# Evidence and experts in two lines each, the router's parts added by a product, and a new plan table in a transformer block

## The chip, the cores and the metric

The kernel runs on one core of a Trainium2 chip. Five engines work side by side: TensorE (PE) multiplies matrices and writes its results to eight PSUM banks; VectorE (DVE) and ScalarE (ACT) work on tiles element by element and read PSUM; GpSimd (POOL) does the same on SBUF alone; SyncE (SP) issues the DMAs. The metric is the time of one execution in microseconds of device time. The kernel before takes 1758.62 us, the median of 3 runs (1758.21 to 1759.53).

## The reference, cut to what matters

Sixteen sequences of 256 tokens with 256 channels go through two layers. All is float32.

```python
# first layer: retrieval from the context, then three experts
nx = layer_norm(x) * gamma + beta
weights = softmax((nx @ Wq) @ (ctx @ Wk).T * 256 ** -0.5)
evidence = weights @ (ctx @ Wv)
combined = concat([nx, evidence, anchor])          # anchor: one vector per sequence
router_probs = softmax(combined @ router_W + router_b)          # 3 experts
h = silu(combined @ e_w1[e] + e_b1[e]);  expert_out[e] = h @ e_w2[e] + e_b2[e]
routed = sum over e of expert_out[e] * router_probs[e]
g = sigmoid(silu(combined @ gate_w1 + gate_b1) @ gate_w2 + gate_b2)
x = x + g * (routed @ out_w + out_b)

# second layer: each part on a normalised x, scaled and shifted by cond, its output gated
x = x + g_msa * self_attention(h)      # 16 heads of 16, windows of 128 rolled by 64
x = x + g_mca * top16_cross_attention(h, ctx)     # the 16 greatest of 256 scores, 16 heads
x = x + g_mlp * ((silu(h @ w_m1[:, :1024]) * (h @ w_m1[:, 1024:])) @ w_m2)
```

## The kernel before, in words

Weights lie in SBUF for the whole run; some are folded into one another first (`folds`, for instance the key weights into the query weights, and the value weights into the router's and the experts' first layers). Activations move through a ring of work buffers (`units`, 128x512 floats each: 26 at first, 76 once the setup's memory is given back by `settled`), a ring of small tiles (`smalls`) and the ring of the eight PSUM banks (`banks`).

The work of a sequence is written as eleven generators, the stages: `evidence` (norm, scores against the context, weights, the gathered evidence, and the router with its probabilities), `experts`, `self_keys`, `self`, `self_out`, `queries`, `keys`, `cross`, `cross_out`, `inputs` and `mlp`. Each yields operations (`Op`): an engine, a duration that the plan reckons with, the tiles that it reads, writes, takes and frees, and a function that issues its instructions. A stage has one line of work, in which it takes sequence 0, 1, 2 and so on (`line`, L1647); `mlp` has two lines, one for the even and one for the odd sequences (`every`, L1671). `after` in the table `STAGES` (L1625) says how far each stage may run ahead of others: `("experts", 2)` lets `evidence` of sequence b begin once `experts` of b - 2 is done. The other numbers of a row are a rank, the work buffers and banks that must stay free beside what a new operation takes, and a window: how many operations the line may have posted at once.

The order of the instructions on every engine is laid down at build time by a planner (`Flow.run`, L235). It keeps a clock for each engine and at each step takes, of all posted operations whose inputs are planned, the one that could begin first; between equals the one with the least time of readiness plus rank:

```python
if op.engine == PE:
    if self.tiled is None:
        rank += op.hold
    elif op.tiled:
        rank -= self.STAY
key = (begin + late, at + rank + late)
```

`tiled` marks the operations that use the array in quarters: the attention scores (`"rows"`, L1382 and L1516: four products of 32 rows at once), the weighted sums and the router's product (`"columns"`, L1337, L1482 and L1107: four products of 32 columns at once). Everything else uses the whole array: products (L565, L576, L1092) and transposes (L493, L1322, L1465, L1117). The planner adds `TURN` to an operation that changes between quarters and whole. While the array is quartered, `STAY` favours quartered operations; while it is whole, `HOLD` puts off the weighted sums. `ASIDE` is what an operation must gain to be moved to its second engine (a PSUM copy from ACT to DVE), `SWITCH` puts off work that needs another table of ACT.

The router's logits are made in parts. Its product (L1103) leaves four partial sums, one for each block of 128 input channels, on four groups of 32 partitions: partition 32k + e holds block k's part for expert e. ACT copies the result to SBUF (L1111), TensorE turns it in two transposes (L1117), VectorE adds the four parts straight from PSUM (`tensor_reduce`, L1133) and adds the router's bias (L1134); then the greatest logit, the shift, the exponential and the division follow (L1137 to L1150).

Sequences 0, 1 and 2 are loaded by the list of `fetches` between the weights; a later one is loaded by its `evidence` when it begins (L1053).

Of the kernel before, what the change touches and what calls it, by code (L numbers as in the profile page):

```python
# [11 lines left out]
ALU = mybir.AluOpType  # L12
AX = mybir.AxisListType
PSUM = bass.MemoryType.PSUM

P = 128
# [31 lines left out]
def t_tr(n):  # L48
    return n * 0.109
# [46 lines left out]
class Op:  # L96
# [5 lines left out]

    def __init__(
        self, engine, us, trace, r=(), w=(), new=(), free=(), table=None, size=0, tiled=None,
        other=(), grain=0.0, hold=0.0,
    ):
        self.hold = hold
# [19 lines left out]
class Flow:  # L127
# [4 lines left out]
    ASIDE = 1.0  # L132
    TURN = 0.093
    SWITCH = 3.0
    STAY = 8.0
    HOLD = 1.0
# [98 lines left out]
    def run(self):  # L235
        while self.works:
# [35 lines left out]
            if op.engine == PE:  # L272
                if (op.tiled is None) != (self.tiled is None):
                    us += self.TURN
                self.tiled = op.tiled
# [23 lines left out]
def pixart_kernel(  # L299
# [29 lines left out]
    for a in range(2):  # L329
        nc.vector.tensor_reduce(mask[:, a : a + 1], iv[:, :, a * D : (a + 1) * D], AX.XY, ALU.add)  # L330

# [156 lines left out]
    def chunks_T(src, free=True, ts=ALL):  # L488

        def trace(pt):  # L490
            for c in range(2):
# [7 lines left out]
                free=(src,) if free else (),  # L499
# [115 lines left out]
    state = [{} for _ in range(B)]  # L615

# [93 lines left out]
    def turned(w, wb, factor=None):  # L710
# [7 lines left out]
        pt = yield from ask(PE, t_tr(4), trace, r=(wb,), new=(banks,))  # L718
# [118 lines left out]
    def conditions():  # L837
# [56 lines left out]
        def by_channels(pm, n):  # L894
# [11 lines left out]
            return (yield from ask(PE, t_tr(2), trace, r=(u,), new=(banks,), free=(u,)))  # L906
# [145 lines left out]
    def evidence(b, s):  # L1052
        if "cx" not in s:  # L1053
            yield from sequence(b, s)
# [46 lines left out]
        def router(pm):  # L1101
# [6 lines left out]
            PE, 0.57, router, r=(nx, ev, *(yield from ready("rw"))), new=(banks,), tiled="columns"  # L1108
# [6 lines left out]
        def turn(pt):  # L1115
            for t in range(NT):
                nc.tensor.transpose(  # L1117
                    pt[:, 0, t * P : (t + 1) * P], u.t[:, 0, t * P : (t + 1) * P], ident
                )
        pt = yield from make(PE, t_tr(2), turn, r=(u,), new=(banks,), free=(u,))  # L1120
# [10 lines left out]
        def shifted(s):  # L1131
            parts = pt.t[:, 0, :].rearrange("p (t k w) -> p t w k", t=NT, w=W)[:, :, 0:E, :]
            nc.vector.tensor_reduce(pr(s), parts, AX.X, ALU.add)  # L1133
            nc.vector.tensor_tensor(  # L1134
                pr(s), pr(s), rb[:, b : b + 1, :].to_broadcast([P, NT, E]), ALU.add
# [4 lines left out]
            DVE, 0.64, shifted, r=(pt, *(yield from ready("rb"))), new=(smalls,), free=(pt,)  # L1140
# [172 lines left out]
    def self_weigh(ts, v, exs, oT, ended):  # L1313

        pTs = []
        for j in range(4 * len(ts)):
# [6 lines left out]
            pt = yield from make(PE, t_tr(4), turn, r=(exs[j],), new=(banks,), free=(exs[j],))  # L1323
# [107 lines left out]
    def cross_weigh(c, t, v, exs, lefts, oT, ended):  # L1431

        pTs = []
        for j in range(4):
# [34 lines left out]
            pt = yield from make(PE, t_tr(4), turn, r=(exs[j],), new=(banks,), free=(exs[j],))  # L1469
# [29 lines left out]
    def cross_attention(b, s, ts):  # L1499
# [3 lines left out]
        for n, (t, c) in enumerate(rounds):  # L1503
# [22 lines left out]
            for j in range(4):  # L1526


                def top(*_, j=j, sc=sc[j], m8s=m8s):
                    for a in range(2):  # L1530
                        nc.vector.max(m8s[j].t[:, 16 * a : 16 * a + 8], sc.t[:, a, :])  # L1531
# [54 lines left out]
    def mlp(b, s, ts):  # L1586
# [39 lines left out]
        ("self_keys", self_keys, 5.0, 2, 2, 4, (("experts", 0), ("self", 1), ("cross", 3))),  # L1626
        ("evidence", evidence, 4.0, 9, 0, 4, (("experts", 2),)),
        ("queries", cross_queries, 3.0, 3, 0, 4, (("self_out", 0), ("cross", 2))),
        ("self", self_attention, 0.0, 4, 0, 24, (("self_keys", 0), ("cross", 3))),
        ("mlp", mlp, 8.0, 4, 0, 6, (("inputs", 0),)),  # L1630
        ("cross_out", cross_output, 1.0, 1, 1, 8, (("cross", 0),)),
        ("cross", cross_attention, 4.0, 2, 1, 24, (("queries", 0), ("keys", 0))),
        ("experts", experts, 7.0, 3, 0, 24, (("evidence", 0), ("self_out", 3))),
        ("inputs", mlp_inputs, 8.0, 6, 1, 24, (("cross_out", 0), ("queries", 0))),
        ("keys", cross_keys, 5.0, 8, 2, 10, (("evidence", 0), ("cross", 1))),
        ("self_out", self_output, 5.0, 1, 1, 6, (("self", 0),)),
# [32 lines left out]
    for name, works, rank, unit, bank, window, after in STAGES:  # L1669

        every = 2 if name == "mlp" else 1  # L1671
# [51 lines left out]
```

## Time and profile before

| what | before |
|---|---|
| median of 3 runs | 1758.62 us |
| the profiled execution, its own time | 1758.5 us |
| its span, first to last instruction | 1756.8 us |
| granted TensorE clock, mean | 0.999 |
| busy: PE, DVE, ACT, POOL | 1726.9, 1398.4, 1162.2, 806.9 us |
| instructions | 36829 |

The profile describes one execution. The span is the time from its first to its last instruction; the execution's own time is 1.7 us more. Busy time is that in which at least one instruction of an engine was under way; register, branch, semaphore and DMA-issuing instructions do not count. The matmuls of PE are pipelined, and their ends are modelled, so two matmul records overlap, and the distance from the start of one to the start of the next tells what it costs. PEld is the weight loads of TensorE, which overlap its matmuls. A float32 product on the whole array or a part of it is two records, a transpose one. "L565" is line 565 of the kernel; many operations go through helpers, so a line can serve many stages, and the names of the tiles tell which. Of a group of waits the profile gives the engine, the tile and the line that waited, whom it waited for, and the time in total, the times and the longest wait. In a line of the timeline the start comes first, then the length, the engine, the line, the operation, its tiles and shape, and how many followed one another.

### The profile page before, as it was taken

What the parts mean: (1) busy time and instruction counts of PE and PEld (TensorE: products, weight loads), DVE (VectorE), ACT (ScalarE), POOL (GpSimd) and SP (SyncE); (2) the same over time, 40 slices, a digit from 0 to 9 for tenths busy, and PEclk for the clock granted to TensorE, in tenths of its full rate; (3) what the DMA queues carried; (4) which work ended last, traced back from release to release, by engine and by line L of the source; (5) the groups of instructions that cost most, each with busy time, mean ns of one, the idle gap of its engine ahead of it and who ended that gap; (6) DMA issues with size and microseconds to landing.
All of it is one profiled execution on the core that took longest, in us unless ns stands there. A gap on an engine that the chain in (4) does not pass through costs nothing. (4 is left out here: it accounts for less than half of the span.)

```text
span 1756.8 us, 36829 instructions
## 1 busy us (share of the span) xinstructions
PE 1726.9 (98%) x12105; PEld 1413.3 (80%) x12105; DVE 1398.4 (80%) x5605; ACT 1162.2 (66%) x3023; POOL 806.9 (46%) x1809
## 2 busy tenths in 40 slices
PE   8999999999999999999999999999999999999998
PEld 6687888888788888788887878888888888878788
DVE  2223878798988986978989989687979888979972
ACT  3336675786787577676676867677776768676641
POOL 1123445545555265443544555535445655453431
PEclk9999999999999999999999999999999999999999
DMA  8300000000000010000000000000000000010101
GB/s 293 127 19 13 1 19 7 7 19 13 25 8 25 1 31 7 7 26 13 26 7 19 7 26 7 7 25 13 19 7 13 14 8 13 26 25 14 25 25 37
DMA packets 33801, 45.11 MB, mean 26 GB/s; under 512 B 5609, under 2 KB 23579, under 8 KB 33099
## 3 DMA queue, kind: packets, MB, share of 16 engines
q1 hardware_dynamic: 33611, 42.77, 7.9%
q8 instruction: 96, 1.57, 0.4%
q14 instruction: 94, 0.77, 0.1%
HBM read 38.46 MB, written 4.30 MB: 24 GB/s over the span
## 5 line engine op out<-in xcount | busy, mean ns | idle before, releaser
L1457 POOL TENSOR_SCALAR u<-u,small 128x256 f32<-128x256 f32 x512 | 251.8, 508 | 307.7 <-DVE small L1450 260.3
L565 PE MATMUL bank<-u,w 128*128 128x256 f32 x1536 | 360.8, 381 | 1.1 <-ACT u L507 0.7
L527 ACT COPY u<-bank 128x512 f32<-128x512 f32 x394 | 227.7, 611 | 156.6 <-PE bank L1465 88.9
L565 PEld LDWEIGHTS bank<-u,w 128*128 128x128 f32 x1536 | 284.7, 190 | 45.4 <-issue 7.3
L1554 ACT ACTIVATE u<-bank,small 128x256 f32<-128x256 f32 x512 | 215.7, 481 | 91.4 <-DVE u L1535 54.4
L565 PE MATMUL bank<-u,wm 128*128 128x256 f32 (+1 forms) x1088 | 248.7, 370 | 1.1 <-ACT u L507 0.7
L1416 POOL TENSOR_SCALAR u<-u,small 128x128 f32<-128x128 f32 x512 | 186.2, 390 | 110.5 <-DVE small L1411 96.2
L565 PEld LDWEIGHTS bank<-u,wm 128*128 128x128 f32 x1088 | 189.8, 190 | 32.7 <-issue 10.0
L1531 DVE MAX8 small<-bank 128x8 f32<-128x256 f32 x512 | 191.8, 415 | 25.9 <-PE bank L1508 25.8
L1535 DVE MATCH_REPLACE8 u<-small,bank 128x256 f32<-128x256 f32 x512 | 207.2, 411 | 0.0
L1573 DVE MATCH_REPLACE8 u<-small,u 128x256 f32<-128x256 f32 x512 | 204.4, 406 | 0.0
L1441 DVE SCALAR_TENSOR_TENSOR u<-u,u 128x256 f32<-128x256 f32 x512 | 203.2, 436 | 0.0
L576 PE MATMUL bank<-w,u 128*128 128x256 f32 x768 | 182.8, 381 | 5.1 <-ACT u L507 5.0
L1566 DVE MAX8 small<-u 128x8 f32<-128x256 f32 x512 | 187.3, 408 | 0.0
L1401 ACT ACTIVATE u<-bank,small 128x128 f32<-128x128 f32 x512 | 180.3, 411 | 10.3 <-DVE small L1392 10.1
L576 PEld LDWEIGHTS bank<-w,u 128*128 128x128 f32 x768 | 141.5, 190 | 25.8 <-ACT u L507 6.6
L1545 POOL TENSOR_SCALAR small<-small 128x2 f32<-128x2 f32 x256 | 55.3, 217 | 225.8 <-DVE small L1531 188.9
L1465 PE MATMUL bank<-ident,u 128*128 128x128 f32 x1024 | 148.0, 275 | 2.9 <-POOL u L1457 0.7
L1465 PEld LDWEIGHTS bank<-ident,u 128*128 128x128 f32 x1024 | 121.0, 141 | 32.1 <-POOL u L1457 7.2
L1401 ACT ACTIVATION_READ_ACCUMULATOR u<-bank,small 128x1 f32 x512 | 128.0, 251 | 0.0
L605 POOL TENSOR_TENSOR u<-u,u 128x256 f32<-128x256 f32 x96 | 70.8, 758 | 106.8 <-DVE u L597 89.7
L507 ACT ACTIVATE u<-bank,prm 128x256 f32<-128x256 f32 (+1 forms) x164 | 69.7, 483 | 73.5 <-PE bank L565 64.3
(172 smaller groups left out, 3094.7 us busy)
## 6 DMA issues: line engine op xcount, KB each, us to landing
u<-gates_d SPq DMA_DIRECT2D x51, 256.0 KB
u<-in_ctx_dram SPq DMA_DIRECT2D x16, 256.0 KB
w<-in_L_xcond_e_w_dram SPq DMA_DIRECT2D x3, 1024.0 KB
wada<-in_L_xcond_w_ada_dram SPq DMA_DIRECT2D x1, 2304.0 KB
u<-in_x_dram SPq DMA_DIRECT2D x16, 128.0 KB
u<-in_x_dram SPq DMA_DIRECT2D x32, 64.0 KB
wm<-in_L_xcond_w_m_dram SPq DMA_DIRECT2D x1, 2048.0 KB
out_dram<-u SPq DMA_DIRECT2D x16, 128.0 KB
```

Source lines behind the costliest of these rows:

```text
L527: ACT, t_copy(512), lambda u: nc.scalar.copy(u, pt.t),
L565: nc.tensor.matmul(to[:, c, cols(ts)], lhsT=w[:, k, col + c * P : col + (c + 1) * P], rhs=rhs[k // 2].t[:, k % 2, cols(ts)], start=start, ...
L576: nc.tensor.matmul(to[:, t, :], lhsT=lhs[k // 2].t[:, k % 2, t * P : (t + 1) * P], rhs=w(k), start=start, stop=stop,)
L1401: nc.scalar.activation(heads4(u)[:, i, :], heads4(sc.t)[:, i, :], AF.Exp, bias=nm.t[:, i : i + 1], accum_out=nm.t[:, 4 + i : 5 + i],)
L1441: nc.vector.scalar_tensor_tensor(ex[:, a, :], left[:, a, :], TAKEN, ex[:, a, :], ALU.is_equal, ALU.mult, accum_out=s[:, a : a + 1],)
L1457: nc.gpsimd.tensor_scalar(ex, ex, sm.t[:, 2 + a : 3 + a], 1.0, ALU.mult, ALU.mult)
L1465: nc.tensor.transpose(heads4(pt)[:, 2 * a + k, :], exs[j].t[:, a, k * P : (k + 1) * P], ident,)
L1531: nc.vector.max(m8s[j].t[:, 16 * a : 16 * a + 8], sc.t[:, a, :])
L1535: nc.vector.match_replace(firsts[j].t[:, a, :], m8s[j].t[:, 16 * a : 16 * a + 8], sc.t[:, a, :], TAKEN,)
L1554: nc.scalar.activation(u[:, a, :], sc.t[:, a, :], AF.Exp, bias=nm.t[:, a : a + 1])
L1566: nc.vector.max(m8s[j].t[:, 16 * a + 8 : 16 * a + 16], firsts[j].t[:, a, :])
L1573: nc.vector.match_replace(left, m8s[j].t[:, 16 * a + 8 : 16 * a + 16], left, TAKEN)
```

## The change

Six things change.

- The router's four parts are added by TensorE: `addup` is a matrix of 128 x 3 with a one where the partition's number modulo 32 is the expert's. Two products of the copied parts with it take the place of the two transposes, and give the sums turned; the reduction on VectorE is gone, and the bias is added straight from PSUM.
- `evidence` and `experts` get two lines each, even and odd sequences, as `mlp` has them. `evidence` of sequences 0 to 2 waits until they are loaded (`LOADED`).
- The router's product is held as the weighted sums are (`hold=flow.HOLD`).
- The planner reckons the way into quarters with `TURN` as before, and the way back with `BACK`: 0.103 before a product, 0.057 before a transpose (`turns`).
- `ASIDE` 1.0 becomes 1.4, `SWITCH` 3.0 becomes 2.0, `STAY` 8.0 becomes 373.0, `HOLD` 1.0 becomes 4.0.
- The table of the stages has other ranks, buffers to keep, windows and lags, and the stages stand in another order.

`top` in the cross attention is written with other arguments and issues the same instructions. The diff, without the five places that only mark a transpose with `turns=True`, and `top`:

```diff
@@ -100,10 +100,12 @@
 
 
 
+
     def __init__(
         self, engine, us, trace, r=(), w=(), new=(), free=(), table=None, size=0, tiled=None,
-        other=(), grain=0.0, hold=0.0,
+        other=(), grain=0.0, hold=0.0, turns=False,
     ):
+        self.turns = turns
         self.hold = hold
         self.grain = grain
         self.tiled = tiled
@@ -129,11 +131,12 @@
 
 
     LOAD = 1.3
-    ASIDE = 1.0
+    ASIDE = 1.4
     TURN = 0.093
-    SWITCH = 3.0
-    STAY = 8.0
-    HOLD = 1.0
+    BACK = 0.103, 0.057
+    SWITCH = 2.0
+    STAY = 373.0
+    HOLD = 4.0
     RATE = 0.31e6
     LAND = 1.7
 
@@ -270,8 +273,10 @@
                 self.table = op.table
                 us += self.LOAD
             if op.engine == PE:
-                if (op.tiled is None) != (self.tiled is None):
+                if op.tiled and self.tiled is None:
                     us += self.TURN
+                elif op.tiled is None and self.tiled:
+                    us += self.BACK[op.turns]
                 self.tiled = op.tiled
             end = begin + us
             if op.grain and op.engine in self.port:
@@ -329,6 +334,12 @@
     for a in range(2):
         nc.vector.tensor_reduce(mask[:, a : a + 1], iv[:, :, a * D : (a + 1) * D], AX.XY, ALU.add)
 
+
+    addup = ct([P, E], "addup")
+    nc.vector.tensor_reduce(
+        addup, ident.rearrange("p (k w) -> p w k", w=2 * D)[:, 0:E, :], AX.X, ALU.add
+    )
+
     prm = ct([P, R_ALL], "prm")
     maskb = ct([P, 4, 2], "maskb")
     qb = ct([P, 4], "qb")
...
@@ -613,6 +624,7 @@
     got, has = {}, {}
     asked = []
     state = [{} for _ in range(B)]
+    LOADED = 3
 
     def loaded(*names):
         while any(name not in got for name in names):
...
@@ -1050,7 +1062,9 @@
         )
 
     def evidence(b, s):
-        if "cx" not in s:
+        while b < LOADED and "x" not in s:
+            yield None
+        if b >= LOADED:
             yield from sequence(b, s)
         cx, xb = s["cx"], s["x"]
         pt = yield from chunks_T(cx, free=False)
@@ -1105,7 +1119,8 @@
                     rhs=s["comb"][k // 2].t[:, k % 2, :], start=True, stop=True,
                 )
         pm = yield from make(
-            PE, 0.57, router, r=(nx, ev, *(yield from ready("rw"))), new=(banks,), tiled="columns"
+            PE, 0.57, router, r=(nx, ev, *(yield from ready("rw"))), new=(banks,), tiled="columns",
+            hold=flow.HOLD,
         )
         u = yield from make(
             ACT, t_copy(256), lambda u: nc.scalar.copy(u[:, 0, :], pm.t[:, 0, :]),
@@ -1114,10 +1129,11 @@
 
         def turn(pt):
             for t in range(NT):
-                nc.tensor.transpose(
-                    pt[:, 0, t * P : (t + 1) * P], u.t[:, 0, t * P : (t + 1) * P], ident
-                )
-        pt = yield from make(PE, t_tr(2), turn, r=(u,), new=(banks,), free=(u,))
+                nc.tensor.matmul(
+                    pt[:, 0, t * E : (t + 1) * E], lhsT=u.t[:, 0, t * P : (t + 1) * P], rhs=addup,
+                    start=True, stop=True,
+                )
+        pt = yield from make(PE, 0.16, turn, r=(u,), new=(banks,), free=(u,))
 
         def pr(s):
             return s[:, 0 : NT * E].rearrange("p (t e) -> p t e", e=E)
@@ -1129,15 +1145,14 @@
             return lm(s).unsqueeze(2).to_broadcast([P, NT, E])
 
         def shifted(s):
-            parts = pt.t[:, 0, :].rearrange("p (t k w) -> p t w k", t=NT, w=W)[:, :, 0:E, :]
-            nc.vector.tensor_reduce(pr(s), parts, AX.X, ALU.add)
             nc.vector.tensor_tensor(
-                pr(s), pr(s), rb[:, b : b + 1, :].to_broadcast([P, NT, E]), ALU.add
+                pr(s), pt.t[:, 0, 0 : NT * E].rearrange("p (t e) -> p t e", e=E),
+                rb[:, b : b + 1, :].to_broadcast([P, NT, E]), ALU.add,
             )
             nc.vector.tensor_reduce(lm(s), pr(s), AX.X, ALU.max)
             nc.vector.tensor_tensor(pr(s), pr(s), each(s), ALU.subtract)
         sm = s["pr"] = yield from make(
-            DVE, 0.64, shifted, r=(pt, *(yield from ready("rb"))), new=(smalls,), free=(pt,)
+            DVE, 0.52, shifted, r=(pt, *(yield from ready("rb"))), new=(smalls,), free=(pt,)
         )
         yield Op(
             ACT, 0.22, lambda: nc.scalar.activation(pr(sm.t), pr(sm.t), AF.Exp), w=(sm,),
...
@@ -1623,17 +1638,17 @@
 
 
     STAGES = (
-        ("self_keys", self_keys, 5.0, 2, 2, 4, (("experts", 0), ("self", 1), ("cross", 3))),
-        ("evidence", evidence, 4.0, 9, 0, 4, (("experts", 2),)),
-        ("queries", cross_queries, 3.0, 3, 0, 4, (("self_out", 0), ("cross", 2))),
-        ("self", self_attention, 0.0, 4, 0, 24, (("self_keys", 0), ("cross", 3))),
-        ("mlp", mlp, 8.0, 4, 0, 6, (("inputs", 0),)),
-        ("cross_out", cross_output, 1.0, 1, 1, 8, (("cross", 0),)),
-        ("cross", cross_attention, 4.0, 2, 1, 24, (("queries", 0), ("keys", 0))),
-        ("experts", experts, 7.0, 3, 0, 24, (("evidence", 0), ("self_out", 3))),
-        ("inputs", mlp_inputs, 8.0, 6, 1, 24, (("cross_out", 0), ("queries", 0))),
-        ("keys", cross_keys, 5.0, 8, 2, 10, (("evidence", 0), ("cross", 1))),
-        ("self_out", self_output, 5.0, 1, 1, 6, (("self", 0),)),
+        ("mlp", mlp, 8.0, 2, 1, 8, (("inputs", 0),)),
+        ("self_keys", self_keys, 2.0, 2, 2, 4, (("experts", 0), ("self", 13), ("cross", 7))),
+        ("cross", cross_attention, 4.0, 0, 1, 6, (("queries", 0), ("keys", 0))),
+        ("self", self_attention, -2.5, 1, 0, 3, (("self_keys", 0), ("cross", 2))),
+        ("experts", experts, 7.0, 4, 0, 8, (("evidence", 0), ("self_out", 2))),
+        ("queries", cross_queries, -4.0, 1, 0, 32, (("self_out", 0), ("cross", 1))),
+        ("self_out", self_output, 2.5, 3, 1, 12, (("self", 0),)),
+        ("evidence", evidence, 5.0, 10, 1, 5, (("experts", 2),)),
+        ("keys", cross_keys, 2.5, 0, 1, 6, (("evidence", 0), ("cross", 1))),
+        ("inputs", mlp_inputs, 8.0, 4, 1, 24, (("cross_out", 0), ("queries", 0))),
+        ("cross_out", cross_output, 3.0, 5, 2, 16, (("cross", 0),)),
     )
     NEEDS = {
         "self_keys": ("wqkv", "mod"), "self_out": ("wso", "gates"),
@@ -1668,7 +1683,7 @@
     flow.add(settled(), 0.0, {}, 8)
     for name, works, rank, unit, bank, window, after in STAGES:
 
-        every = 2 if name == "mlp" else 1
+        every = 2 if name in ("mlp", "experts", "evidence") else 1
         for first in range(every):
             flow.add(
                 line(name, works, after, every, first), rank, {units: unit, banks: bank}, window
```

More of the change, by code (lines that the diff above doesn't have):

```diff
@@ L498, in chunks_T @@
                 PE, t_tr(2 * len(ts)), trace, r=(src,), new=(banks,),
-                free=(src,) if free else (),
+                free=(src,) if free else (), turns=True,
             )
@@ L717, in trace @@
                     )
-        pt = yield from ask(PE, t_tr(4), trace, r=(wb,), new=(banks,))
+        pt = yield from ask(PE, t_tr(4), trace, r=(wb,), new=(banks,), turns=True)
         def out(u):
@@ L905, in trace @@
                     )
-            return (yield from ask(PE, t_tr(2), trace, r=(u,), new=(banks,), free=(u,)))
+            return (yield from ask(PE, t_tr(2), trace, r=(u,), new=(banks,), free=(u,), turns=True))
         def add(dst, pt, g, n, r):
@@ L1322, in turn @@
                     nc.tensor.transpose(heads4(pt)[:, i, :], heads4(exs[j].t)[:, i, :], ident)
-            pt = yield from make(PE, t_tr(4), turn, r=(exs[j],), new=(banks,), free=(exs[j],))
+            pt = yield from make(PE, t_tr(4), turn, r=(exs[j],), new=(banks,), free=(exs[j],), turns=True)
             pT = yield from copied(pt)
@@ L1468, in turn @@
                         )
-            pt = yield from make(PE, t_tr(4), turn, r=(exs[j],), new=(banks,), free=(exs[j],))
+            pt = yield from make(PE, t_tr(4), turn, r=(exs[j],), new=(banks,), free=(exs[j],), turns=True)
             pT = yield from copied(pt)
@@ L1526, in cross_attention, with top @@
             for j in range(4):
-                def top(*_, j=j, sc=sc[j], m8s=m8s):
+                def top(m8, sc=sc[j]):
                     for a in range(2):
-                        nc.vector.max(m8s[j].t[:, 16 * a : 16 * a + 8], sc.t[:, a, :])
+                        nc.vector.max(m8[:, 16 * a : 16 * a + 8], sc.t[:, a, :])
                 def take(*_, j=j, sc=sc[j], firsts=firsts, m8s=m8s):
```

## The prediction

> **What bounds the kernel now.** I read the page first: the busy shares, then the slices.
>
> ```profile
> span 1756.8 us, 36829 instructions
> PE 1726.9 (98%) x12105; PEld 1413.3 (80%) x12105; DVE 1398.4 (80%) x5605; ACT 1162.2 (66%) x3023; POOL 806.9 (46%) x1809
> DVE  2223878798988986978989989687979888979972
> ```
>
> TensorE is busy 98% of the span, VectorE 80%, and VectorE has almost nothing to do in the first four slices and the last. So the question is what TensorE's time is made of. By stages, with the busy time of PE third and that of DVE fifth among the engines' figures:
>
> ```profile
> core 0: us, PE busy (x) PEld busy (x) DVE busy (x) ACT busy (x) POOL busy (x), PEclk, DMA share, GB/s
> 0.00:176.00 176.00, 162.62 (x894) 127.72 (x895) 46.67 (x139) 73.35 (x182) 34.38 (x80) 0.99 0.34 113
> 176.00:1581.00 1405.00, 1395.14 (x10081) 1144.13 (x10079) 1219.50 (x4917) 1001.77 (x2662) 710.37 (x1606) 1.00 0.05 15
> 1581.00:1669.00 88.00, 87.19 (x597) 70.49 (x596) 87.97 (x386) 56.92 (x115) 37.55 (x81) 1.00 0.08 19
> 1713.00:1757.00 44.00, 38.73 (x243) 35.49 (x241) 9.64 (x26) 8.34 (x24) 7.09 (x10) 1.00 0.12 37
> ```
>
> TensorE's idle time is 13.4 us up to 176, 9.9 us in the 1405 after that, 0.8 in the next 88, and 5.3 in the last 44, where nothing is left to multiply after the last product. VectorE idles 185 us in the long middle, but not at all from 1581 to 1669. The granted clock is 0.99 to 1.00 throughout, so no part of the sum needs a clock term.
>
> Busy TensorE is not TensorE at its peak, so I added up the starts of its records. In undisturbed rows a 256-column record takes 216 ns to the next start, a 128x128 transpose 109 ns, a record on a quarter of the array (scores, weighted sums, the router's product) a quarter of its columns' time. By these prices the 12105 records cost 1637 us. The other 120 us are what the change can reach: about 71 us lie around the stretches in which the array is quartered, 45 us elsewhere (waits, the start, the end). One such stretch:
>
> ```profile
> 316.53 0.38 PE L1322 MATMUL bank<-ident,u 128*128 128x128 f32 x2
> 316.84 1.08 PE L1297 MATMUL bank<-u,v 128*32 128x128 f32 x32
> 317.85 1.15 PE L1375 MATMUL bank<-u,u 32*128 32x256 f32 x16
> 318.93 0.70 PE L576 MATMUL bank<-w,u 128*128 128x256 f32 x2
> ```
>
> Two transposes should end at 316.75; the sums start at 316.84 (0.09 lost). Sums and scores should take 0.87 + 0.86 and take 2.09 (0.36 lost); the first whole record after them takes 0.32 instead of 0.22 (0.10 lost). There are 158 such stretches. Medians: scores alone lose 0.40 us, column work alone 0.34, one of each in one stretch 0.55, two column operations in one stretch 0.35. So joining a column stretch to scores saves 0.40 + 0.34 - 0.55 = 0.20, and to another column stretch 0.34 + 0.34 - 0.35 = 0.33.
>
> **The change, part by part.**
>
> *The router's parts by a product with ones.* Removed: 2 transposes per sequence and one VectorE reduction from PSUM (16 x 0.166 = 2.7 us). Added: two products of 3 columns. Neither lies in the trace at this place, but the folding has the same form, and the transposes are there:
>
> ```profile
> 13.06 0.95 PE L730 MATMUL bank<-rw,u 128*128 128x3 f32 x8
> 13.89 0.48 PE L576 MATMUL bank<-u,u 128*128 128x256 f32 x1
> 30.49 0.38 PE L1117 MATMUL bank<-ident,u 128*128 128x128 f32 x2
> 30.71 0.60 PE L493 MATMUL bank<-ident,u 128*128 128x128 f32 x4
> ```
>
> The eight records are four products (whole f32 products come as two records; transposes as one). They hold PE for 0.83 us, 0.112 apart after the first, the spacing of their weight loads. Four records cost 0.83 - 4 x 0.112 = 0.38, the two transposes 0.22: +0.16 x 16 = **+2.6 us**. Bounds: -1.0 (the plan's own 0.16 in place of 0.22) and +3.7 (0.112 for all four). I take +2.6, the same form and weight size. The page "Perfetto Trace Analysis" of the Trainium skill (Optimizing Tensor Performance, Transposes) advises the transpose over a standard matmul for a transposition, which speaks against this edit. "TensorEngine Tiling (Array Packing)" (Performance Considerations, Instruction Overhead) says that a product of one column costs as much as one of 60; by that, an estimate of 60/256 x 0.216 = 0.05 per record gives 0.20 for four and a term of -0.3 in place of +2.6. VectorE's 2.7 us I count at nothing: its 185 us of idle time cover it; were VectorE the bound, they would be a gain of 2.7. The matrix of ones is one small VectorE reduction before 4 us, while PE waits 3.7 us for its first weights: nothing.
>
> *STAY 8 to 373.* In a quartered stretch the plan now leaves only when no quartered operation can start at once. That saves only where one was passed over. After a stretch the next one starts within 2 us once in 157 times, so there was practically none: **0**, and the same at both ends.
>
> *HOLD 1 to 4, the router's product included.* In whole mode a column operation may now be passed by work up to 4 us younger (3 us more than before; the router's, 4 more). 73 stretches begin with column work; the next stretch begins within 4 us of the end of 13 of them, within 5 of 18, within 8 of 36. I take 15 joined at a mean of 0.25: **-3.8 us**. Bounds: 0, and -12 (36 x 0.33). What queues behind a held sum is its copy on ACT and then the output product of the attention; a held router delays its copy, the softmax and the experts. Router to experts is 24 us and more from the third sequence on (155 to 179, 190 to 265), which covers 4.
>
> *Evidence and experts in two lines.* No instruction is added. Before, the second sequence's evidence could begin only when the first's was over: its router ran at 107, the first's at 27. PE's waits up to 176:
>
> ```profile
> PE bank L576 <- ACT u L507: 4.5, 2, 3.6
> PE bank L715 <- DMA wq<-in_L_xcond_Wq_dram: 3.7, 1, 3.7
> PE bank L1117 <- ACT u L1111: 2.2, 2, 1.7
> ```
>
> The first and third are one sequence alone in its own chain (a second layer waiting for its SiLU, the router's turn waiting for its copy), which a companion can cover: 6.7 us; the DMA's 3.7 stays. I take **-5**; bounds -9.7 (13.4 less 3.7) and +5, since until the weights' folding is done only 26 work buffers exist for two sequences, and the later wait of 2.2 could double. In the middle the same SiLU waits are 2.4 + 1.4; I take **-2.5** of these 3.8. The new wait for a loaded sequence holds the evidence of sequences 0 to 2 alone, which the list of fetches loads anyway. SP issues the same loads, two sequences' sooner; queues at 5% of the DMA engines there cover them, and a late context would cost its landing before an evidence that runs many us ahead.
>
> *Ranks, lags, windows, ASIDE, SWITCH, BACK.* These only reorder. What they could recover in the middle is the 9.9 us of idle, part of it used above; what they could lose has no row. I take **0**, with bounds -6 (9.9 less 3.8) and +12 (the 88 us of full VectorE, see below). The tail stays: the gate, the add and the store after the last product are untouched.
>
> **Sum.** 2.6 - 3.8 - 5 - 2.5 = -8.7 against the profiled execution's 1758.5 (span 1756.8 and 1.7 around it), which stands 0.1 under the median of 1758.62: **1750 us**. A change within 0.2% (3.5 us) is what this kernel's measurement can hardly tell from none.
>
> **The rivals.**
>
> *VectorE becomes the bound late (slower).* Pairing at the start spends PE time on evidence and experts before attention begins. First self scores run at 142 us, and experts 0 take 71 to 119. One sequence's experts are 84 products (three times 16 + 8, and 8 + 4 for the gate) of 0.432 = 36 us of PE. Both sequences' experts can overlap only in part, since the second waits for its own evidence; if attention starts a third of 36, 12 us, later, VectorE has 12 us less for its 1352 us after 176, and whole products that filled PE beside it at 1581 to 1669 are already spent. For: VectorE is full there, with no reserve. Against: 185 us of VectorE idle before. It decides where the delay is not made up by 1581; then up to 12 us come back as PE idle, and +2.6 with them: 1758.5 + 14.6 = 1773; with half of it, 1758.5 + 6 + 2.6 = 1767.
>
> *Grouping does more than I count (faster).* With lags wider for the self keys (13 for 1) sums and scores of different sequences meet more often: 36 joined at 0.33 = -12 and all 9.7 at the start, with -2.5 in the middle and +2.6: 1737. Against: eight banks, four of them taken by each scores operation.
>
> *It moves nothing.* Joins are undone by new ones split elsewhere and the start is set by the weights: +2.6 -3.8 and nothing else: 1757.
>
> **How the numbers follow.** Forecast 0.45, more grouping 0.15, nothing 0.10, late VectorE 0.30. The forecast's own range is 1742 to 1755. To leave out no more than 2 in 10, the whole range takes in the grouping rival down to 1738 and the slow case up to 1769, past the middle of the slow case. Faster: 0.45 + 0.15 = 0.60; same: 0.09, slower 0.31 (the slow case and a tenth of the unmoved one).
>
> **What would show it.** The router's products: four 3-column records per sequence about 0.112 apart, and no reduction behind them. Grouping: some 143 quartered stretches in place of 158, and the time around them near 67 us in place of 71. Start: the second router's product well before 107, and the 4.5 and 2.2 us of waits gone from the first 176. Wrong if quartered stretches stay near 158, or if PE idles in the last 180 us while VectorE is full; the first scores of the first sequence well after 142 and VectorE's share over 90% in the middle would announce that.

## The result and the profile after

The changed kernel takes 1736.34 us, the median of 4 runs (1736.12 to 1736.46), against 1758.41 us before (1758.18 to 1759.53): the ratio is 0.9875, with a 95% interval of 0.9863 to 0.9888. It is 22 us faster; the prediction said 1750, with a range from 1738 to 1769.

The page of the changed kernel, the lines that answer to those shown before:

```profile
span 1734.5 us, 36952 instructions
PE 1714.7 (99%) x12137; PEld 1422.4 (82%) x12137; DVE 1395.0 (80%) x5605; ACT 1170.2 (67%) x3020; POOL 812.2 (47%) x1809
DVE  2215598978979798987868898999799999889992
```

The span fell by 22.3 us and PE's busy time by 12.2, so 10.1 us of the gain were idle time of PE, and the rest was time in which its records lay further apart than they need without a gap between them. The stages, same columns as before:

```profile
core 0: us, PE busy (x) PEld busy (x) DVE busy (x) ACT busy (x) POOL busy (x), PEclk, DMA share, GB/s
0.00:176.00 176.00, 169.91 (x908) 135.85 (x909) 51.09 (x150) 73.83 (x203) 35.54 (x83) 1.00 0.33 110
176.00:1559.00 1383.00, 1374.65 (x10107) 1140.96 (x10106) 1208.80 (x4901) 1003.24 (x2630) 714.17 (x1600) 1.00 0.05 15
1559.00:1647.00 88.00, 88.00 (x573) 74.59 (x573) 80.34 (x337) 55.71 (x113) 30.85 (x68) 1.00 0.07 19
1691.00:1734.50 43.50, 38.47 (x301) 34.88 (x299) 10.77 (x32) 8.58 (x25) 10.72 (x17) 0.98 0.11 31
```

PE's idle time up to 176 us fell from 13.4 to 6.1 us, and in the middle from 9.9 to 8.4. VectorE is half busy in the fourth slice now, where it had 3 tenths before, but also in the fifth, where it had 8: the first self scores come at 155 us in place of 142. PE's waits up to 176:

```profile
PE bank L727 <- DMA wq<-in_L_xcond_Wq_dram: 3.8, 1, 3.8
PE bank L587 <- ACT u L538: 1.3, 2, 0.7
PE bank L576 <- ACT u L518: 0.4, 1, 0.4
```

Line 518 here is line 507 of the kernel before, 576 and 587 are its 565 and 576. The wait for the first weights stands; the 4.5 us for the SiLU and the 2.2 us for the router's copy are gone or shrunk to 0.4. Waits of 1.3 us for a PSUM copy (L538) are new.

To see where the rest went, I did the prediction's sum again for every run below. Each record of PE is priced by undisturbed rows (216 ns for 256 columns on the whole array, a quarter of that on a quarter of it, 109 ns for a transpose, and 70 ns for a 3-column record). What the starts of the records take beyond that is put down to the place where it falls: *around the stretches* is from the last whole record before a quartered stretch to the second one after it, waits there included; *start* is the rest up to 176 us, *end* the rest of the last 88 us, *middle* what lies between. "Idle" is PE's idle time up to 176 us in the windows. All in us; "time" is the median of a kernel's runs, and the other columns come from the trace of its profiled execution. The columns from "around" to "end" and the price of the records (1637 or 1638) add up to the span.

| kernel | time | span | stretches | around | start | middle | end | idle to 176 |
|---|---|---|---|---|---|---|---|---|
| before | 1758.4 | 1756.8 | 158 | 71.5 | 20.8 | 20.6 | 7.2 | 13.4 |
| after | 1736.3 | 1734.5 | 124 | 61.1 | 12.5 | 16.3 | 7.0 | 6.1 |
| after, transposes in the router | 1737.8 | 1736.3 | 124 | 61.7 | 12.8 | 18.2 | 7.0 | 6.4 |
| before, products in the router | 1758.7 | 1758.1 | 158 | 70.9 | 22.1 | 20.2 | 7.2 | 13.2 |
| after, TURN 0.094 | 1763.3 | 1761.6 | 124 | 71.8 | 12.5 | 21.5 | 18.2 | 6.2 |
| before, HOLD 5 | 1763.8 | 1762.4 | 127 | 66.0 | 22.6 | 30.7 | 6.4 | 13.7 |
| after, HOLD 1 | 1763.1 | 1761.4 | 164 | 71.7 | 11.9 | 31.5 | 8.7 | 5.7 |
| after, HOLD 1, own table | 1746.4 | 1744.0 | 158 | 67.7 | 11.7 | 20.1 | 6.9 | 5.6 |
| after, one line each | 1789.3 | 1787.2 | 127 | 76.4 | 17.9 | 35.4 | 19.8 | 14.7 |
| after, one line each, own table | 1760.1 | 1756.4 | 119 | 67.7 | 18.5 | 25.6 | 6.9 | 15.5 |
| after, two lines for evidence only | 1774.3 | 1773.8 | 126 | 61.9 | 19.0 | 34.7 | 20.5 | 9.1 |
| after, two lines for experts only | 1800.1 | 1798.3 | 129 | 86.1 | 17.9 | 34.0 | 22.6 | 16.4 |
| before, LOAD 1.32 | 1774.2 | 1770.6 | 158 | 79.9 | 19.3 | 25.6 | 9.2 | 14.2 |
| after, STAY 8 | 1737.4 | 1735.6 | 125 | 62.2 | 12.1 | 16.6 | 7.0 | 6.5 |

By the first two rows the change is worth 10.4 us around the stretches (158 became 124), 8.3 at the start, 4.3 in the middle, 0.2 at the end, less 1.0 for the new records: 22.2.

### The profile page after: what moved, and what is told of

Same layout as the page of the kernel before. It is cut to its first block, busy times and chain, and to the rows that moved or that the text cites. A ratio compares the mean times of both kernels' runs of the same rounds, so it can differ in the third digit from the quotient of the medians.

```text
span 1734.5 us, 36952 instructions
## 1 busy us (share of the span) xinstructions
PE 1714.7 (99%) x12137; PEld 1422.4 (82%) x12137; DVE 1395.0 (80%) x5605; ACT 1170.2 (67%) x3020; POOL 812.2 (47%) x1809
## 4 chain that ended last, share of the span: by engine, by line
PE 73%; DVE 18%; ACT 5%; issue 2%; POOL 1%; DMA 0%; SPq 0%; POOLq 0%; DVEq 0%; ACTq 0%
PE bank L576 33%; PE bank L587 18%; PE bank L1480 4%; PE bank L1312 4%; DVE u L1550 4%; DVE small L1546 3%; DVE u L1588 3%; DVE u L1456 3%; PE bank L1523 3%; PE bank L1337 3%; DVE small L1581 3%; PE bank L504 2%; PE bank L742 2%; PE bank L1390 1%; ACT u L1416 1%
## 5 line engine op out<-in xcount | busy, mean ns | idle before, releaser
L1472 POOL TENSOR_SCALAR u<-u,small 128x256 f32<-128x256 f32 x512 | 262.1, 526 | 334.6 <-DVE small L1465 298.9
L538 ACT COPY u<-bank 128x512 f32<-128x512 f32 x396 | 229.0, 620 | 113.5 <-PE bank L1480 66.4
L1480 PE MATMUL bank<-ident,u 128*128 128x128 f32 x1024 | 145.7, 275 | 3.7 <-POOL u L1472 1.8
L1480 PEld LDWEIGHTS bank<-ident,u 128*128 128x128 f32 x1024 | 119.6, 141 | 30.2 <-POOL u L1472 10.5
L1416 ACT ACTIVATION_READ_ACCUMULATOR u<-bank,small 128x1 f32 x512 | 132.0, 266 | 0.0
L518 ACT ACTIVATE u<-bank,eb 128x256 f32<-128x256 f32 x192 | 79.3, 474 | 70.9 <-PE bank L576 67.6
L587 PE MATMUL bank<-wm,u 128*128 128x256 f32 x512 | 116.1, 380 | 0.0
```

Source lines behind the costliest of these rows:

```text
L538: ACT, t_copy(512), lambda u: nc.scalar.copy(u, pt.t),
L587: nc.tensor.matmul(to[:, t, :], lhsT=lhs[k // 2].t[:, k % 2, t * P : (t + 1) * P], rhs=w(k), start=start, stop=stop,)
L1416: nc.scalar.activation(heads4(u)[:, i, :], heads4(sc.t)[:, i, :], AF.Exp, bias=nm.t[:, i : i + 1], accum_out=nm.t[:, 4 + i : 5 + i],)
L1472: nc.gpsimd.tensor_scalar(ex, ex, sm.t[:, 2 + a : 3 + a], 1.0, ALU.mult, ALU.mult)
L1480: nc.tensor.transpose(heads4(pt)[:, 2 * a + k, :], exs[j].t[:, a, k * P : (k + 1) * P], ident,)
```

## The experiments

Two theories were to be told apart. The first is the prediction's: the gain is the sum of the parts (joined stretches, two lines at the start, the router). The second: the planner lays out one order among very many, the new table was one that happened to fit, and the parts alone explain little.

**The router's product, with the order kept.** In the changed kernel:

```diff
-                nc.tensor.matmul(
-                    pt[:, 0, t * E : (t + 1) * E], lhsT=u.t[:, 0, t * P : (t + 1) * P], rhs=addup,
-                    start=True, stop=True,
+                nc.tensor.transpose(
+                    pt[:, 0, t * P : (t + 1) * P], u.t[:, 0, t * P : (t + 1) * P], ident
                 )
...
+            parts = pt.t[:, 0, :].rearrange("p (t k w) -> p t w k", t=NT, w=W)[:, :, 0:E, :]
+            nc.vector.tensor_reduce(pr(s), parts, AX.X, ALU.add)
             nc.vector.tensor_tensor(
-                pr(s), pt.t[:, 0, 0 : NT * E].rearrange("p (t e) -> p t e", e=E),
-                rb[:, b : b + 1, :].to_broadcast([P, NT, E]), ALU.add,
+                pr(s), pr(s), rb[:, b : b + 1, :].to_broadcast([P, NT, E]), ALU.add
             )
```

> The changed kernel with two transposes and VectorE's reduction back in place of the two products with ones. The plan still reckons with the products' figures, so the order on every engine stays as it is. The prediction's term (+0.16 us for each of 16 sequences) expects 2.6 us less than the changed kernel, some 1733.7 us. The rival, that the products cost what the plan says (0.16 in place of 0.22), expects 1.0 us more, some 1737.3 us.

It took 1737.78 us (1737.72 to 1738.1), 1.4 more than the changed kernel; the spans say 1.8 more. The times of the two do not overlap, but they were not taken side by side, and the intervals of their ratios to the kernel before, 0.9863 to 0.9888 and 0.9868 to 0.9895, overlap. So the 2.6 us that the transposes were to save did not come, and whether the products pay, by little, is not settled. In place they do not pay. One of them in the changed kernel's timeline, and the same place with the transposes (PE alone; start, length, line):

```profile
75.87 0.50 PE L1132 MATMUL bank<-addup,u 128*128 128x3 f32 x4
76.23 1.11 PE L576 MATMUL bank<-u,w 128*128 128x256 f32 x4
```

```profile
76.16 0.38 PE L1132 MATMUL bank<-ident,u 128*128 128x128 f32 x2
76.37 0.81 PE L576 MATMUL bank<-u,w 128*128 128x256 f32 x3
```

The four records hold PE for 0.36 us, the two transposes for 0.21; the record after the products takes 0.30 to the next start instead of 0.22. Over the 16 routers, from the record before to the second one after, the transposes are 2.8 us shorter. But both kernels issue the other 12073 records of PE in the same order, so they can be laid side by side, and outside the routers the one with transposes loses 4.8 us. Of these 0.6 lie ahead of the first router, where the two do the same, and 2.8 in steps of up to 0.5 us in front of the transposes of attention weights (L1480 and L1337). At some of them the trace shows PE, which got there sooner, waiting. That VectorE's extra reduction is what it waited for, 16 times 0.166 us and whatever queues behind it, is the obvious reading, but it is argued and not shown.

**The same, in the kernel before.**

```diff
-                nc.tensor.transpose(
-                    pt[:, 0, t * P : (t + 1) * P], u.t[:, 0, t * P : (t + 1) * P], ident
+                nc.tensor.matmul(
+                    pt[:, 0, t * E : (t + 1) * E], lhsT=u.t[:, 0, t * P : (t + 1) * P], rhs=addup,
+                    start=True, stop=True,
                 )
         pt = yield from make(PE, t_tr(2), turn, r=(u,), new=(banks,), free=(u,))
...
```

(and `addup` made, the reduction on VectorE left out and the bias added from PSUM, as in the changed kernel).

> The kernel before with the products with ones alone; the plan keeps the transposes' figures, so nothing else moves. The prediction's term expects 2.6 us more than before, 1761.0 us; the plan's figure expects 1.0 us less, 1757.4 us.

1758.68 against 1758.82 us of the kernel before beside it, a ratio of 0.9999 (0.9990 to 1.0008). The 2.6 us more that the prediction expected lie outside; a gain of 1 and none cannot be told apart.

**A thousandth of a microsecond in the plan.** In the changed kernel:

```diff
-    TURN = 0.093
+    TURN = 0.094
```

> The changed kernel with one thousandth of a microsecond more for the way into quarters in the plan's reckoning (0.093 to 0.094). No instruction, lag, rank or window differs; the laid-out order has as many quartered stretches. If the gain comes from the parts of the change (grouping, two lines, the router), the time stays within 2 us of 1736. If it comes from one well-chosen order out of many that the same parts allow, this order is a different one and loses most of the gain: over 1746 us, with the loss in waits of TensorE and not around the quartered stretches (61 us).

1763.27 us: 27 us slower than the changed kernel, slower than the kernel before (ratio 1.0025, 1.0015 to 1.0035). TensorE has the same records, and its stretches are 124 as well. Their order is the changed kernel's up to 503 us, and another one from there on. With the order other things move: ScalarE loads its tables 200 times in place of 172, at 1.28 us each. Of the 27 us, 21 are lost in the last 88: 11 of them stand under "end" in the table, and most of the 10.7 that "around" grew by are waits in that end as well, beside its stretches. The last 132 us of this kernel, by windows:

```profile
1586.00:1674.00 88.00, 86.75 (x596) 72.12 (x598) 82.90 (x353) 58.63 (x117) 34.67 (x79) 1.00 0.06 16
1674.00:1718.00 44.00, 33.70 (x196) 23.69 (x192) 43.94 (x194) 17.78 (x38) 19.87 (x45) 0.81 0.09 25
1718.00:1762.00 44.00, 36.67 (x309) 32.75 (x300) 19.36 (x78) 15.89 (x40) 12.12 (x21) 0.97 0.10 25
```

and the matching 44 us of the changed kernel:

```profile
1647.00:1691.00 44.00, 43.62 (x255) 36.12 (x254) 43.97 (x190) 28.81 (x53) 20.91 (x44) 1.00 0.13 37
```

VectorE is full in both (the fifth figure). In the changed kernel PE has other work beside it and idles 0.4 us; in the other it idles 10.3 us, and the granted clock falls to 0.81. The waits in that window:

```profile
PE bank L1480 <- POOL u L1472: 8.2, 2, 4.8
```

L1480 turns the cross attention's weights once VectorE and POOL have made them. The last sequence's first cross scores start at 1659 us here and at 1613 in the changed kernel, so VectorE's chain ends later, with too few products left to put beside it: from 1674 on this kernel has 256 records of the MLP, while the changed kernel has 374 in its last 88 us. Whether the added table loads delay that chain is not shown. The kernels below with one line each and with two lines for experts only end in the same way, with VectorE at 43 to 44 of 44 us and clocks of 0.81 and 0.84:

```profile
1699.00:1743.00 44.00, 36.30 (x186) 25.56 (x184) 42.71 (x186) 19.57 (x42) 16.98 (x39) 0.81 0.06 19
1711.00:1755.00 44.00, 31.46 (x213) 22.85 (x212) 44.00 (x200) 24.09 (x46) 17.77 (x41) 0.84 0.04 13
```

**Holding alone, in the kernel before.**

```diff
-    HOLD = 1.0
+    HOLD = 5.0
```

> The kernel before with the holding of weighted sums raised from 1 to 5 and nothing else (with 4 it cannot be laid out). Its order has 31 quartered stretches fewer (of the same count that falls by 34 in the change). If grouping is worth its price by itself, 31 x 0.3 = 9 us less than before: 1749 us, with 62 us around the stretches in place of 71. If the order decides, the 9 us around the stretches are gained all the same and given back as waits: 1753 to 1765 us.

1763.78 us, ratio 1.0022 (1.0012 to 1.0031): slower. The stretches fell to 127 and the time around them by 5.5 us (9 were expected), but the middle lost 10.1. The waits of PE in the whole kernel begin as before and go on with many small ones:

```profile
PE bank L576 <- ACT u L507: 6.4, 5, 3.6
...
PE bank L565 <- ACT u L507: 2.9, 3, 1.2
PE bank L1117 <- ACT u L1111: 2.2, 2, 1.7
PE bank L493 <- DVE u L1602: 1.7, 1, 1.7
PE bank L1465 <- ACT u L507: 1.6, 4, 1.0
```

In this table the longer hold gives back more than it gains.

**No holding, in the changed kernel.**

```diff
-    HOLD = 4.0
+    HOLD = 1.0
```

> The changed kernel with the holding of column work back at 1 in place of 4; everything else as changed. Its order has 41 more quartered stretches. If HOLD is what joins the stretches, the time around them rises from 61 to some 72 us, the idle time of TensorE up to 176 us stays at 6 us, and the total is some 1748 us. If the new table, not HOLD, did the joining, the time around the stretches stays near 61 us. What goes beyond 1752 us would be an end in which VectorE is full and TensorE waits, as with the thousandth of a microsecond.

1763.12 us, 27 more than the changed kernel. The stretches are 164 and the time around them 71.7, just what HOLD alone should do; the start keeps its gain (idle 5.7). The rest, 15 us, is in the middle, not at the end as I had thought.

**One line each, in the changed kernel.**

```diff
-        every = 2 if name in ("mlp", "experts", "evidence") else 1
+        every = 2 if name == "mlp" else 1
```

> The changed kernel with one line each for evidence and experts. Its order has 3 quartered stretches more than the changed kernel's. If the two lines bring the start, the idle time of TensorE up to 176 us rises from 6 to some 13 us as before the change, and the total by 7 to some 1743 us. If the start comes from the table, it stays at 6 us. Beyond 1748 us the middle or the end is worse, which the windows show.

1789.29 us. The idle time up to 176 us is 14.7, as expected of the start; middle and end lose another 32 us, and so do the stretches, 15, with waits in them. So the lines bring the start, but the sum of the parts misses the total by far.

**The kernel before with two hundredths in the plan.**

```diff
-    LOAD = 1.3
+    LOAD = 1.32
```

> The kernel before with two hundredths of a microsecond more for a table load of ScalarE in the plan's reckoning (1.30 to 1.32); no instruction differs, and the number of quartered stretches is the same. If the kernel before was an ordinary order, the time moves by less than 4 us either way around 1758. If it was itself a well-chosen one, it gets slower by over 6 us, above 1765 us, with the time around the stretches within 2 us of 71.

1774.21 us, ratio 1.0086 (1.0071 to 1.0101), with as many stretches and the same records of TensorE, in another order from 974 us on. ScalarE loads its tables less often here, 152 times in place of 160, so more loads are not what makes this order slower. By this one trial the kernel before was a well-fitting order too. The time around the stretches did not stay at 71 but rose to 79.9, by waits that fall into them, among them one of 3.5 us for POOL.

After these seven runs neither theory stands alone. A fair comparison needs a table chosen for each version. The next two kernels have one, chosen among some 2500 small variations of the changed table by the end that the plan reckons.

**HOLD 1 and STAY 8 with their own table.** The core of it:

```diff
-    STAY = 373.0
-    HOLD = 4.0
+    STAY = 8.0
+    HOLD = 1.0
...
-        ("queries", cross_queries, -4.0, 1, 0, 32, (("self_out", 0), ("cross", 1))),
+        ("queries", cross_queries, -3.5, 1, 0, 33, (("self_out", 0), ("cross", 1),)),
-        ("self", self_attention, -2.5, 1, 0, 3, (("self_keys", 0), ("cross", 2))),
+        ("self", self_attention, -2.5, 3, 0, 3, (("self_keys", 0), ("cross", 2),)),
-        ("cross_out", cross_output, 3.0, 5, 2, 16, (("cross", 0),)),
+        ("cross_out", cross_output, 1.0, 5, 2, 16, (("cross", 0),)),
```

(and another order of the rows).

> The changed kernel with HOLD 1 and STAY 8 as before the change, but with its own table, chosen among some 2500 small variations of the changed one for the earliest end that the plan reckons. Its order has some 35 more quartered stretches than the changed kernel's. If joining is worth its 10 us by itself and the 15 us that HOLD 1 lost in the middle were only a table that did not fit, some 71 us are spent around the stretches, start 12, middle and end back near 23: 1745 to 1749 us. If holding is what keeps the middle free of waits, the middle stays over 28 and the total over 1752 us.

1746.42 us, ratio 0.9923 (0.9908 to 0.9938): as the first theory expects, 10 us slower than the changed kernel, and 14 faster than the kernel before beside it (1760.34). Middle and end are back at 27. So most of the 15 us that HOLD 1 lost in the middle were a table that did not fit, and between these two tables holding (with `STAY`) is worth 10 us; a better table for HOLD 1 is not ruled out. 6.6 of these lie around the stretches, 3.8 in the middle. The start keeps its gain here too, in contrast to the kernel with one line each that follows. The first 176 us of this kernel and of that one:

```profile
0.00:176.00 176.00, 170.39 (x916) 136.97 (x917) 51.95 (x154) 72.65 (x208) 37.25 (x87) 1.00 0.33 111
```

```profile
0.00:176.00 176.00, 160.50 (x873) 126.71 (x874) 43.75 (x133) 71.51 (x178) 32.94 (x79) 0.97 0.33 110
```

**One line each with its own table.** The core of it:

```diff
-        every = 2 if name in ("mlp", "experts", "evidence") else 1
+        every = 2 if name == "mlp" else 1
...
-    ASIDE = 1.4
-    HOLD = 4.0
+    ASIDE = 1.35
+    HOLD = 5.5
...
-        ("mlp", mlp, 8.0, 2, 1, 8, (("inputs", 0),)),
+        ("mlp", mlp, 9.0, 2, 1, 16, (("inputs", 0),)),
-        ("evidence", evidence, 5.0, 10, 1, 5, (("experts", 2),)),
+        ("evidence", evidence, 5.0, 8, 1, 5, (("experts", 2),)),
...
```

(and other figures in the rows of `self_keys`, `self`, `inputs` and `queries`, and another order of the rows).

> The changed kernel with one line each for evidence and experts, and its own table (and HOLD 5.5, ASIDE 1.35), chosen in the same way among some 2500 variations. If two lines bring the start alone, the start is 18 to 21 us in place of 12.5, the time around the stretches some 60, middle and end near 23: 1742 to 1746 us. If they also keep the middle and the end free of waits, those stay over 30 together and the total over 1750 us.

1760.12 us, ratio 1.0002 (0.9993 to 1.0012): no better than the kernel before, and 24 us behind the changed one. The start's waits are back:

```profile
PE bank L587 <- ACT u L518: 7.3, 2, 6.1
PE bank L727 <- DMA wq<-in_L_xcond_Wq_dram: 3.7, 1, 3.7
```

The wait of 6.1 us falls into a quartered stretch, so the table counts it there: start and stretches together are 12.6 us worse than in the changed kernel with 5 stretches fewer. The middle is 9.3 us worse; with the end it comes to 32.5, as the expectation's second way has it. Whether that is the missing second line or a table not as well chosen as the changed one, the runs don't settle.

**STAY 8 in the changed kernel.**

```diff
-    STAY = 373.0
+    STAY = 8.0
```

> The changed kernel with STAY 8 in place of 373. Its order has one quartered stretch more. The prediction's term of nothing expects 1736 us within 2; if a long stay joins the stretches, it is slower by the price of its splits, and if the order is as touchy as with the thousandth of a microsecond, by over 10 us.

1737.35 us, 1.0 more. The stay does next to nothing, as predicted: 12113 of the 12137 records of TensorE stand where they stood. So this run does not test how touchy the order is.

**Which of the two lines.**

```diff
-        every = 2 if name in ("mlp", "experts", "evidence") else 1
+        every = 2 if name in ("mlp", "evidence") else 1
```

> The changed kernel with two lines for evidence and one for experts. If an early second evidence is what fills the start, TensorE's idle time up to 176 us stays at 6 us; if the second line of experts is, it is 13 to 15 us as with one line each. The total is over 1750 us in either case, since the table was not chosen for this order.

```diff
-        every = 2 if name in ("mlp", "experts", "evidence") else 1
+        every = 2 if name in ("mlp", "experts") else 1
```

> The changed kernel with two lines for experts and one for evidence. If an early second evidence fills the start, the idle time up to 176 us is 13 to 15 us; if the second line of experts does, it is 6 us. The total is over 1750 us in either case, since the table was not chosen for this order.

1774.27 and 1800.14 us. The first 176 us of the first and of the second:

```profile
0.00:176.00 176.00, 166.89 (x908) 131.42 (x909) 47.30 (x138) 76.44 (x190) 39.09 (x90) 0.98 0.33 110
```

```profile
0.00:176.00 176.00, 159.60 (x871) 125.20 (x872) 40.15 (x123) 76.26 (x186) 37.88 (x87) 0.98 0.33 110
```

Idle are 9.1 and 16.4 us, against 14.7 with one line each. The second line of evidence fills most of the idle time of the start; a second line of experts without it finds, by this reading, no second sequence ready, and beside it brings the last 3 us (9.1 to 6.1). Idle time is not all: with everything that the records lose up to 176 us, stretches and lower clocks included (0.97 or 0.98 in place of 1.00), the losses are 31.8 us with one line each, 26.0 with two for evidence, 32.7 with two for experts and 17.8 with both. So the second line of evidence alone brings under half of the start's gain, and the pair the whole. Both totals are far above, with ends of 20 us and more: the changed table does not suit them.

With the two lines alone in the kernel before, and with the old table in the changed kernel, the planner comes to a point at which no operation can go on. The new table alone in the kernel before (with `top` as the changed kernel has it) was not run. So what the table is worth by itself stays open. No kernel here beats the changed one.

## Why the prediction was right and wrong

The direction was right, and so was the nature of the gain: idle time at the start, joined stretches, an unmoved end. The size was not: -8.7 was forecast, -22.1 measured. By the table's first two rows the 13.5 us between -8.7 and its -22.2 are 6.6 in the term of HOLD, 3.3 in the start, 1.8 in the middle, 1.6 in the router's products (the price of their records is +1.0, not +2.6) and 0.2 at the end. The sum by its terms:

- *The router's products, +2.6.* Right in place (2.8 over the 16 routers), wrong in total: in the kernel before they cost nothing that can be told from noise, and undoing them in the changed kernel saves nothing. The step that failed here is "VectorE's 2.7 us I count at nothing: its 185 us of idle time cover it", by the obvious reading: what PE loses in the router with the products, it is spared elsewhere in small waits. That TensorE is busy 99% of the time does not mean that a shorter TensorE path shortens the kernel by as much. The advice of the Trainium skill's "Perfetto Trace Analysis" (Optimizing Tensor Performance, Transposes) to use the transpose agrees with the price in place, 0.21 against 0.36 us, and does not show in the total here. The estimate from "TensorEngine Tiling (Array Packing)" (Performance Considerations, Instruction Overhead), 0.05 us for a 3-column record, does not hold: three of the four take 0.11 to the next start.
- *STAY, 0.* Right: 1.0 us. Its reason was misread: after a stretch the next one starts within 2 us 13 times, not once (see HOLD).
- *HOLD, -3.8.* This is the term that made the forecast miss: of the 13.5 us, 6.6 are its own. By the first rows of the table it is -10.4, and by the run with its own table -10, of which 6.6 lie around the stretches. Its mechanism held: without it the stretches are back at 164, and the time around them at 71.7. The step that failed is the count of joins, 15. The prediction says that 13, 18 and 36 stretches of column work have their successor within 4, 5 and 8 us of their end; in the trace these are the counts from their start. From the end they are 21, 28 and 44. The one pair that it found within 2 us shows it, in the kernel before:

```profile
315.25 0.64 PE L1103 MATMUL bank<-u,rw 128*32 128x256 f32 x8
315.82 0.55 PE L493 MATMUL bank<-ident,u 128*128 128x128 f32 x3
```

  The next stretch begins at 316.84, 1.59 us after the start of this one and 1.02 after its end. By the right counts some 24 joins at 0.25, an estimate in the prediction's own way, would be -6. But 34 went, at 0.31 each. The code shows why more went: HOLD is added to the rank, and the ranks differ. A sum of the cross attention (4 + 4) gives way to work of the self attention (-2.5) that became ready up to 10.5 us later, and of the queries (-4) up to 12. The prediction read HOLD as a time, when it is a term in a comparison that the new ranks move as well. The upper bound, -12, held it, though by the right counts it would have been -14.5.
- *Two lines at the start, -5.* Right in cause and near in size: -7.3 idle, -8.3 with the gaps between records. The upper bound was 9.7.
- *Two lines in the middle, -2.5.* -4.3, of which the runs cannot say how much is the lines and how much the table.
- *Ranks, lags and windows, 0.* In balance small: before and after have ends of like size, and the middles differ by the 4.3 above. But the bounds, -6 and +12, were far too narrow for what such a change could have done. A thousandth in TURN costs 27 us, one line each 53. This step priced the new table as a reshuffle with an even chance. The seven runs that lay out another order in a table not chosen for it (TURN, LOAD, both of HOLD, one line each, two lines for one stage) are 5 to 64 us slower than the kernel they were made from; so the new table seems as well fitted as the old was.

Of the rivals, "Grouping does more than I count" came out at 1737, 0.7 us from the measurement, with the chance of 0.15; its terms were -12, -9.7, -2.5 and +2.6 against -10.4, -8.3, -4.3 and +1.0. That it came so close is luck in part: it has too much for the first two and too little for the others. "VectorE becomes the bound late" did not happen to the changed kernel, where VectorE is full from 1647 to 1691 and PE beside it too, although the sign that the prediction named for it came in part: the first scores stand 13 us later, at 155. It happened in four of the experiments (TURN, one line each, two lines for one stage), at 11 to 16 us more in the end's column and with clocks down to 0.81. It is one way for an order to be bad; the runs with HOLD 1, HOLD 5 and LOAD lose in the middle or around the stretches. The deciding point named in the prediction, a delay not made up by 1581, was too coarse: by these runs it matters whether products are left over for the last attention.

Two more figures of the prediction want setting right. Its "45 us elsewhere" leave out the 3.7 us before the first record; the table has 48.6. And the other signs it named came out beyond it: 124 stretches for 143, 61 us around them for 67, and the second router's product at 70 us in place of 107.

## What to carry to other kernels

When a planner lays out the order, its figures are part of the program: a change of a thousandth in one of them cost more here than the whole edit brought. Compare two versions when each has its own chosen table, and read the parts of a gain by place (start, switches, middle, end) instead of by undoing one line. An engine that is busy 99% of the time can still wait in small pieces, so a price in place is not yet a price in total; and of a slack engine, ask at its fullest stretch, not on average, whether it covers the work.

## What the runs showed of the hardware

The granted clock fell to 0.81 in the 44 us in which PE idled 10.3 (TURN 0.094). Among the records of the last 88 us, those of the cross scores took 805 ns in the mean there, and 640 in the last 88 us of the changed kernel:

```profile
L1523 PE MATMUL bank<-u,u 32*128 32x512 f32 x24 | 4.4, 805 | 0.0
```

```profile
L1523 PE MATMUL bank<-u,u 32*128 32x512 f32 x16 | 2.3, 640 | 0.0
```

So the end with waits was paid twice in this run, in idle time and in slower records. And the way out of a quartered stretch is not the same for all: the first whole product's record after it takes 320 ns to the next start in place of 216, the first transpose 165 in place of 109, in the kernel before as in the changed one. These are the 0.103 and 0.057 of `BACK`. The way in costs 93 ns before either: the last record ahead of a stretch takes 309 ns for a product and 202 for a transpose.
